# Products of each row with itself: rows at multiples of 256 bytes, and stores on two queues

## The chip, the cores and the metric

The kernel runs on one core of one Trainium2 chip. The metric is the device time of one execution in microseconds (us); where a kernel was run several times, it is their median. One further execution is taken with the hardware profiler, and the profile and its trace come from that one.

## The reference

The input `x` has 4096 rows of 256 float32 numbers. For each row, all products of two of its elements are formed, and those of the upper triangle (diagonal included) are written out, row of the triangle by row:

```python
B, D = (4096, 256)
d = inputs.shape[1]
dot = jnp.einsum('bi,bj->bij', inputs, inputs)
iu, ju = jnp.triu_indices(d)
return dot[:, iu, ju]
```

The result has 4096 rows of 256 * 257 / 2 = 32,896 float32 numbers. That is 539 MB to be written, from 4.2 MB that are read, with one multiplication per number written.

## The kernel before, in words

**Tiling.** Each of the 128 partitions takes 32 consecutive rows of `x`. They are worked on two at a time (`REPEAT`), so there are 16 groups of 128 x 2 rows. The 32,896 products of a row are cut at multiples of `UNIT` = 32 into three pieces (`PIECES`) of 10,944, 10,976 and 10,976 columns. A store thus moves one piece of one group: 128 partitions, two rows in each, 43,776 or 43,904 contiguous bytes per row. The whole work is 48 such pieces, numbered `p`; `p % 3` is the piece within the group.

**Places.** A piece is built in one of two buffers in SBUF, the places `o0` and `o1`: even `p` in the first, odd `p` in the second. Each has the form 128 x 2 x `slot`, with `slot` = 10,976, so the second row lies 43,904 bytes after the first. A place can only be refilled when its store has landed. The tile pool lays out, in this order, all of `x` (128 x 8192), `xv` (a working copy of the group's two rows, one element longer), `xa` (a copy for ScalarE), and the places.

**Who computes.** A triangle row `i` is `x[i]` times the contiguous stretch `x[i:]`, for both rows of the partition in one instruction. VectorE multiplies `xv` by `xp` (a copy of the same rows in PSUM, L220), GpSimd multiplies `xv` by itself (L272). Within a piece, GpSimd takes the tail that its cost formula puts at no more than 19.4 us (`BUDGET`), and VectorE takes the rest. `blocks` makes this division. Before the first piece of a group VectorE copies `x` into `xv` and `xp` (L199).

**The head.** The first two pieces (`AHEAD`) are shared by VectorE and ScalarE instead (L244), GpSimd being absent from them. The first piece is cut at 512, 1536, 3584 and 6400 columns (`FIRST`) and stored in five parts, so that the first transfer can begin early. ScalarE first makes its own copy `xa` (L239). Its work ends with these two pieces. From `p` = 2 on each engine runs a loop of eight passes over six pieces.

**Order of the work.** There is no scheduler; semaphores written by hand order the engines:

- SyncE issues the three loads of `x` and then, in the order of `p`, every store. Ahead of a store it waits for one increment of `v_done` (VectorE's part is done) and one of `a_done` or `g_done` (the other engine's part is done). The function is `sync`, the waits are L295 and L296, the issue is L298. All loads and stores therefore stand in one DMA queue.
- When a store has landed, the semaphore `free0` or `free1` of its place rises by 16. VectorE waits for it before it refills the place, and then releases GpSimd through `go` (L207 and L210).
- The five parts of the first piece count on `head`; TensorE waits for all of them and passes this on to `free0`.
- A group's first piece may overwrite `xv` only when GpSimd has read it (`x_read`).
- `take` (L163, L164) waits for a value and subtracts it again.

At the end SyncE waits for the last stores (L338), for `x_read` and for the three loads.

Of the kernel before, what the change touches and what calls it, by code (L numbers as in the profile page):

```python
# [1 line left out]

# [6 lines left out]
F32 = mybir.dt.float32  # L9
AF = mybir.ActivationFunctionType  # L10
ALU = mybir.AluOpType

P = 128
UNIT = 32
REPEAT = 2
PIECES = 3
PLACES = 2
SETS = 2
PASS = 6
# [94 lines left out]
def kernel(  # L114
# [15 lines left out]
    nc = tc.nc  # L130
# [12 lines left out]
    x_out = out.rearrange("(p h q r) c -> h q p r c", p=P, q=rounds, r=REPEAT)  # L143

    pool = ctx.enter_context(tc.tile_pool(name="all", bufs=1))
    xt = pool.tile([P, passes, rounds * each], F32, name="x")

    xv = pool.tile([P, each + 1], F32, name="xv")
    xa = pool.tile([P, each], F32, name="xa")

    xp = ctx.enter_context(tc.tile_pool(name="psum", bufs=1, space=bass.MemoryType.PSUM)).tile([P, each], F32, name="xp")
    places = [pool.tile([P, REPEAT, slot], F32, name=f"o{k}") for k in range(PLACES)]
    ctx.enter_context(tc.tile_critical())  # L153

    def semaphore(name: str):
        return ctx.enter_context(nc.semaphore(name))

    free = [semaphore(f"free{k}") for k in range(PLACES)]
    head, v_done, a_done, go = (semaphore(s) for s in ("head", "v_done", "a_done", "go"))
    loads = [0, each, groups // 2 * each, groups * each]  # L160
    loaded = [semaphore(f"loaded{k}") for k in range(len(loads) - 1)]

    def take(engine, sem, value: int):  # L163
        engine.wait_ge(sem, value).then_inc(sem, -value)  # L164

    v_own, a_own, g_own = (semaphore(s) for s in ("v_own", "a_own", "g_own"))
    g_done, x_read = semaphore("g_done"), semaphore("x_read")

    def x_of(h, q: int) -> bass.AP:
        return xt[:, bass.ds(h, 1), q * each : (q + 1) * each].rearrange("p o d -> p (o d)")  # L170
# [21 lines left out]
    def vector(h, pieces: range, ahead: bool, done: int = 0) -> int:  # L192
        for p in pieces:
            place = places[p % PLACES]
            if p % PIECES == 0:
                if not ahead:
                    take(nc.vector, x_read, 1)
                for to in (xv[:, :each], xp):
                    ins = nc.vector.tensor_copy(to, x_of(h, p // PIECES))  # L199
                    if done:  # L200
                        ins._wait_ge(v_own, done)
                    ins.then_inc(v_own, 1)
                    done += 1
                nc.vector.wait_ge(v_own, done)
            if not ahead:
                if use(p) < uses:
                    nc.vector.wait_ge(free[p % PLACES], 16 * use(p)).then_inc(go, 1)  # L207
                else:
                    take(nc.vector, free[p % PLACES], 16 * uses)
                    nc.vector.sem_inc(go, 1)  # L210
            for _, _, _, block, lo in blocks(p, ahead):
                order = interleave(block)

                own = (p + 1) % PIECES == 0 or p == pieces[-1]
                waits = schedule(order)
                counted = {*waits.values(), *([len(order) - 1] if own else [])}
                number = {k: done + 1 + c for c, k in enumerate(sorted(counted))}
                for k, ((i, j, at, length), m, _) in enumerate(order):
                    at -= lo
                    ins = nc.vector.tensor_tensor(  # L220
                        place[:, :, at : at + m * length],
                        window(xv[:, j:], [[d, REPEAT], [1, m], [1, length]]),
                        window(xp[:, i:], [[d, REPEAT], [1, m], [0, length]]),
                        ALU.mult,
                    )
                    if k in waits:
                        ins._wait_ge(v_own, number[waits[k]])
                    if k in counted:
                        ins.then_inc(v_own, 1)
                done += len(counted)  # L230
                if own:
                    nc.vector.wait_ge(v_own, done).then_inc(v_done, 1)
                else:
                    ins.then_inc(v_done, 1)
        return done

    def scalar(pieces: range):

        nc.scalar.activation(xa, x_of(0, 0), AF.Copy).then_inc(a_own, 1)  # L239
        take(nc.scalar, a_own, 1)  # L240
        for p in pieces:
            for _, _, block, _, lo in blocks(p, True):
                todo = [
                    nc.scalar.activation(  # L244
                        places[p][:, r, at - lo : at - lo + length],
                        xa[:, r * d + j : r * d + j + length],
                        AF.Copy,
                        scale=xa[:, r * d + i : r * d + i + 1],
                    )
                    for i, j, at, length in block  # L250
                    for r in range(REPEAT)
                ]
                if todo:
                    todo[-1].then_inc(a_done, 1)
                else:
                    nc.scalar.sem_inc(a_done, 1)

    def gpsimd(h, pieces: range, ahead: bool):

        done = turns = 0  # L260
        for p in () if ahead else pieces:
            place = places[p % PLACES]
            ((_, _, block, _, lo),) = blocks(p, False)
            turns += 1
            nc.gpsimd.wait_ge(go, turns)
            order = interleave(block)
            waits = schedule(order)
            counted = {len(order) - 1, *waits.values()}
            number = {k: done + 1 + c for c, k in enumerate(sorted(counted))}
            for k, ((i, j, at, length), m, _) in enumerate(order):  # L270
                at -= lo
                ins = nc.gpsimd.tensor_tensor(  # L272
                    place[:, :, at : at + m * length],
                    window(xv[:, j:], [[d, REPEAT], [1, m], [1, length]]),
                    window(xv[:, i:], [[d, REPEAT], [1, m], [0, length]]),
                    ALU.mult,
                )
                if k in waits:
                    ins._wait_ge(g_own, number[waits[k]])
                if k in counted:  # L280
                    ins.then_inc(g_own, 1)
            done += len(counted)
            nc.gpsimd.wait_ge(g_own, done).then_inc(g_done, 1)
            if (p + 1) % PIECES == 0:
                nc.gpsimd.sem_inc(x_read, 1)
        if turns:
            nc.gpsimd.sem_inc(g_own, -done)
            nc.gpsimd.sem_inc(go, -turns)

    def sync(h, pieces: range, ahead: bool):  # L290
        for p in pieces:
            place = places[p % PLACES]
            parts = list(blocks(p, ahead))
            for lo, hi, *_, base in parts:
                take(nc.sync, v_done, 1)  # L295
                take(nc.sync, a_done if ahead else g_done, 1)  # L296
                to = x_out[bass.ds(h, 1), p // PIECES, :, :, base + lo : base + hi]
                nc.sync.dma_start(to.rearrange("o p r c -> p (o r) c"), place[:, :, lo:hi]).then_inc(  # L298
                    free[p % PLACES] if len(parts) == 1 else head, 16
                )  # L300

    def all_pieces(engine, pieces_of):
        done = pieces_of(0, range(AHEAD), True)
        if engine is nc.vector:
            nc.vector.sem_inc(v_own, -done)
        if engine is not nc.sync:
            for sem in loaded[1:]:
                engine.wait_ge(sem, 16)
        kind = engine.engine
        with nc.Fori(  # L310
            0,
            passes,
            engines=OrderedEngineSet([kind]),
            head_slot={kind: 0} if engine is not nc.sync else {},
        ) as h:
            done = pieces_of(h, range(AHEAD, PASS), False)
            with engine.If(h < passes - 1):
                nxt = nc.s_assert_within(h + 1, 0, passes - 1)
                if engine is nc.vector:
                    nc.vector.sem_inc(v_own, -vector(nxt, range(AHEAD), False, done))  # L320
                else:
                    pieces_of(nxt, range(AHEAD), False)
        if engine is nc.vector:
            nc.vector.sem_inc(v_own, -done)
# [7 lines left out]
    take(nc.tensor, head, 16 * (len(FIRST) + 1))  # L332
    nc.tensor.sem_inc(free[0], 16)
    scalar(range(AHEAD))
    for engine, pieces_of in ((nc.vector, vector), (nc.gpsimd, gpsimd), (nc.sync, sync)):
        all_pieces(engine, pieces_of)
    for k in range(PLACES):
        take(nc.sync, free[k], 16 * uses)  # L338
    take(nc.sync, x_read, 1)
    for sem in loaded:  # L340
        take(nc.sync, sem, 16)


# [25 lines left out]
```

## Time and profile before

| | |
|---|---|
| Median of 3 runs | 1270.35 us (1270.26 to 1270.40) |
| Profiled execution: its span, first to last instruction | 1268.8 us |
| VectorE busy | 794.1 us, 63% |
| GpSimd busy | 767.8 us, 61% |
| ScalarE busy (head only) | 29.9 us, 2% |
| DMA moved | 543 MB, 428 GB/s on average |

The profiled execution is known by its span alone; no other time of it is on record. The page of a profile gives the busy time of each engine, then the span in 40 equal slices (a digit is the busy share of an engine in tenths, the line GB/s is what the DMA moved), the DMA queues, the chain of work that ended last, the costliest groups of instructions with what they waited for, and the DMA issues with the median time from issue to landing. In names such as `DVE o L220 <- DMA out_dram<-o` the first part is an engine (DVE is VectorE, POOL is GpSimd, ACT is ScalarE, SP is SyncE), what it writes and the line of the kernel, and after the arrow comes what ended its wait. Behind the page stands the trace, with a record of each instruction and of each DMA packet. In this kernel a packet of a store is one row of one partition. A table of windows gives the same busy times for chosen stretches of the span; the last two columns are the share of time in which the DMA engines were busy, and the GB/s.

### The profile page before, as it was taken

The page shows a single profiled execution, that of the slowest core. Times are in us where ns is not written, and L with a number is a line of the kernel's source. Part 1 is how long each engine was busy: PE and PEld are TensorE (multiplying, and loading weights), DVE is VectorE, ACT ScalarE, POOL GpSimd, SP SyncE. Part 2 cuts the span into 40 slices and gives each one's busy share as a digit, 9 for nine tenths or more (in the row PEclk, how much of TensorE's full clock was granted, in tenths as well). Part 3 has the DMA queues.
Part 4 walks back from the last instruction along what each step waited for, and adds up shares of the span by engine and source line. Part 5 has one row for each costly group of instructions (what it writes and reads, how often), then busy time and mean ns, then how long its engine had stood idle before and what let it go on. Part 6 is the DMA issues. An engine that isn't in the chain of part 4 may idle for free. (4 is left out here: it accounts for less than half of the span.)

```text
span 1268.8 us, 3000 instructions
## 1 busy us (share of the span) xinstructions
DVE 794.1 (63%) x1197; ACT 29.9 (2%) x80; POOL 767.8 (61%) x1032
## 2 busy tenths in 40 slices
DVE  8756856567466674766648665486655866468560
ACT  9000000000000000000000000000000000000000
POOL 0467674676647765577556765567656675576750
DMA  9999999999999999999999999999999999999997
GB/s 379 438 437 425 439 431 433 434 428 433 431 435 429 437 426 438 426 437 424 439 425 439 427 436 429 435 430 433 430 433 428 435 421 441 421 442 421 438 425 336
DMA packets 14583, 543.22 MB, mean 428 GB/s; under 512 B 880, under 2 KB 880, under 8 KB 1520
## 3 DMA queue, kind: packets, MB, share of 16 engines
q1 hardware_dynamic: 14576, 543.17, 99.5%
q14 instruction: 7, 0.06, 0.0%
HBM read 4.19 MB, written 538.97 MB: 428 GB/s over the span
## 5 line engine op out<-in xcount | busy, mean ns | idle before, releaser
L272 POOL TENSOR_TENSOR o<-xv 128x292 f32<-128x292 f32 (+60 forms) x1028 | 767.6, 787 | 461.8 <-DVEq L207 322.1
L220 DVE TENSOR_TENSOR o<-xv,xp 128x512 f32<-128x512 f32 (+61 forms) x1164 | 776.1, 746 | 429.4 <-DMA out_dram<-o 303.8
L244 ACT ACTIVATE o<-xa 128x253 f32<-128x253 f32 (+38 forms) x78 | 27.9, 454 | 0.2 <-ACTq L164 0.2
L199 DVE COPY xv<-x 128x512 f32 (+1 forms) x16 | 6.8, 427 | 10.0 <-DVEq L164 7.2
L199 DVE COPY xp<-x 128x512 f32 (+1 forms) x16 | 11.1, 695 | 0.6
L239 ACT ACT_TABLE_LOAD x1 | 1.3, 1283 | 0.9 <-SPq L153 0.9
L328 DVE MEMSET xv<- 128x1 f32 x1 | 0.1, 59 | 1.0 <-SPq L153 1.0
L239 ACT ACTIVATE xa<-x 128x512 f32<-128x512 f32 x1 | 0.6, 631 | 1.7 <-DMA x<-in_r_inputs_dram 1.7
L356 POOL MEMSET const-float32-0.0<- 128x1 f32 x1 | 0.1, 98 | 0.2 <-issue 0.2
L356 POOL MEMSET const-bfloat16-1.0<- 128x1 bf16 x1 | 0.1, 101 | 0.0
L356 POOL MEMSET const-uint8-127<- 128x1 uint8 x1 | 0.1, 101 | 0.0
L356 POOL MEMSET const-float32-1.0<- 128x1 f32 x1 | 0.1, 98 | 0.0
## 6 DMA issues: line engine op xcount, KB each, us to landing
out_dram<-o SPq DMA_DIRECT2D x32, 10976.0 KB, 32.1
out_dram<-o SPq DMA_DIRECT2D x15, 10944.0 KB, 33.6
out_dram<-o SPq DMA_DIRECT2D x1, 4544.0 KB, 19.4
out_dram<-o SPq DMA_DIRECT2D x1, 2816.0 KB, 15.1
x<-in_r_inputs_dram SPq DMA_DIRECT2D x1, 2048.0 KB, 12.4
out_dram<-o SPq DMA_DIRECT2D x1, 2048.0 KB, 12.6
x<-in_r_inputs_dram SPq DMA_DIRECT2D x1, 1792.0 KB, 7.1
out_dram<-o SPq DMA_DIRECT2D x1, 1024.0 KB, 9.7
```

The source lines that it names most:

```text
L199: ins = nc.vector.tensor_copy(to, x_of(h, p // PIECES))
L220: ins = nc.vector.tensor_tensor(place[:, :, at : at + m * length], window(xv[:, j:], [[d, REPEAT], [1, m], [1, length]]), window(xp[:, i:] ...
L239: nc.scalar.activation(xa, x_of(0, 0), AF.Copy).then_inc(a_own, 1)
L244: nc.scalar.activation(places[p][:, r, at - lo : at - lo + length], xa[:, r * d + j : r * d + j + length], AF.Copy, scale=xa[:, r * d + i ...
L272: ins = nc.gpsimd.tensor_tensor(place[:, :, at : at + m * length], window(xv[:, j:], [[d, REPEAT], [1, m], [1, length]]), window(xv[:, i:] ...
L328: nc.vector.memset(xv[:, each:], 0.0)
L356: nc = _bacc.Bacc("TRN2", target_bir_lowering=False, num_devices=1)
```

## The change

The change has these parts:

- `UNIT` goes from 32 to 64 columns, so that pieces start and end at multiples of 256 bytes: 10,944, 10,944 and 11,008 columns. `slot` becomes 11,008, so the rows of a place are 44,032 bytes apart.
- An unused tile of 32 columns, `edge`, is laid out first, then the places, then `x` and `xv`. The places with it are to start at multiples of 256 bytes.
- ScalarE's copy `xa` is dropped; in the head it reads `x` itself.
- `v_done`, `a_done` and `g_done` become two semaphores each, one per place.
- `sync` becomes `store`, which takes an engine and a place. SyncE issues the stores of the first place, ScalarE, once its part of the head is done, those of the second, on its own DMA queue. ScalarE thus also runs the loop of eight passes.
- Of the waits at the end, those for the last stores come last.

```diff
-UNIT = 32
+UNIT = 64
 REPEAT = 2
 PIECES = 3
+EDGE = 32
...
+    pool.tile([P, EDGE], F32, name="edge")
+    places = [pool.tile([P, REPEAT, slot], F32, name=f"o{k}") for k in range(PLACES)]
     xt = pool.tile([P, passes, rounds * each], F32, name="x")
-
     xv = pool.tile([P, each + 1], F32, name="xv")
-    xa = pool.tile([P, each], F32, name="xa")
...
-    places = [pool.tile([P, REPEAT, slot], F32, name=f"o{k}") for k in range(PLACES)]
...
-    head, v_done, a_done, go = (semaphore(s) for s in ("head", "v_done", "a_done", "go"))
+    head, go = semaphore("head"), semaphore("go")
+    v_done, a_done, g_done = ([semaphore(f"{s}{k}") for k in range(PLACES)] for s in ("v_done", "a_done", "g_done"))
...
-        nc.scalar.activation(xa, x_of(0, 0), AF.Copy).then_inc(a_own, 1)
-        take(nc.scalar, a_own, 1)
+        xa = xt[:, 0, :each]
...
-    def sync(h, pieces: range, ahead: bool):
+    def store(engine, k: int, h, pieces: range, ahead: bool):
         for p in pieces:
-            place = places[p % PLACES]
+            if p % PLACES != k:
+                continue
+            place = places[k]
             parts = list(blocks(p, ahead))
             for lo, hi, *_, base in parts:
-                take(nc.sync, v_done, 1)
-                take(nc.sync, a_done if ahead else g_done, 1)
+                take(engine, v_done[k], 1)
+                take(engine, (a_done if ahead else g_done)[k], 1)
                 to = x_out[bass.ds(h, 1), p // PIECES, :, :, base + lo : base + hi]
-                nc.sync.dma_start(to.rearrange("o p r c -> p (o r) c"), place[:, :, lo:hi]).then_inc(
-                    free[p % PLACES] if len(parts) == 1 else head, 16
+                engine.dma_start(to.rearrange("o p r c -> p (o r) c"), place[:, :, lo:hi]).then_inc(
+                    free[k] if len(parts) == 1 else head, 16
                 )
...
     scalar(range(AHEAD))
-    for engine, pieces_of in ((nc.vector, vector), (nc.gpsimd, gpsimd), (nc.sync, sync)):
+    stores = [(engine, partial(store, engine, k)) for k, engine in enumerate((nc.sync, nc.scalar))]
+    for engine, pieces_of in ((nc.vector, vector), (nc.gpsimd, gpsimd), *stores):
         all_pieces(engine, pieces_of)
-    for k in range(PLACES):
-        take(nc.sync, free[k], 16 * uses)
     take(nc.sync, x_read, 1)
     for sem in loaded:
         take(nc.sync, sem, 16)
+    for k in range(PLACES):
+        take(nc.sync, free[k], 16 * uses)
```

More of the change, by code (lines that the diff above doesn't have):

```diff
@@ L1 @@
 from contextlib import ExitStack
+from functools import partial
 import concourse.bass as bass
@@ L164, in take @@
         engine.wait_ge(sem, value).then_inc(sem, -value)
-    v_own, a_own, g_own = (semaphore(s) for s in ("v_own", "a_own", "g_own"))
-    g_done, x_read = semaphore("g_done"), semaphore("x_read")
+    v_own, g_own = (semaphore(s) for s in ("v_own", "g_own"))
+    x_read = semaphore("x_read")
     def x_of(h, q: int) -> bass.AP:
@@ L231, in vector @@
                 if own:
-                    nc.vector.wait_ge(v_own, done).then_inc(v_done, 1)
+                    nc.vector.wait_ge(v_own, done).then_inc(v_done[p % PLACES], 1)
                 else:
-                    ins.then_inc(v_done, 1)
+                    ins.then_inc(v_done[p % PLACES], 1)
         return done
     def scalar(pieces: range):
-        nc.scalar.activation(xa, x_of(0, 0), AF.Copy).then_inc(a_own, 1)
-        take(nc.scalar, a_own, 1)
+        xa = xt[:, 0, :each]
         for p in pieces:
@@ L253, in scalar @@
                 if todo:
-                    todo[-1].then_inc(a_done, 1)
+                    todo[-1].then_inc(a_done[p % PLACES], 1)
                 else:
-                    nc.scalar.sem_inc(a_done, 1)
+                    nc.scalar.sem_inc(a_done[p % PLACES], 1)
     def gpsimd(h, pieces: range, ahead: bool):
@@ L282, in gpsimd @@
             done += len(counted)
-            nc.gpsimd.wait_ge(g_own, done).then_inc(g_done, 1)
+            nc.gpsimd.wait_ge(g_own, done).then_inc(g_done[p % PLACES], 1)
             if (p + 1) % PIECES == 0:
@@ L305, in all_pieces @@
             nc.vector.sem_inc(v_own, -done)
-        if engine is not nc.sync:
+        if engine in (nc.vector, nc.gpsimd):
             for sem in loaded[1:]:
@@ L313, in all_pieces @@
             engines=OrderedEngineSet([kind]),
-            head_slot={kind: 0} if engine is not nc.sync else {},
+            head_slot={kind: 0} if engine in (nc.vector, nc.gpsimd) else {},
         ) as h:
```

## The prediction

> **What bounds the kernel now.** I read the page first (busy shares, slices, queues), then the table of windows, the DMA view of the last 89 us, the waits and the chain.
>
> ```profile
> DMA  9999999999999999999999999999999999999997
> ...
> q1 hardware_dynamic: 14576, 543.17, 99.5%
> ...
> out_dram<-o SPq DMA_DIRECT2D x32, 10976.0 KB, 32.1
> ```
>
> The 16 DMA engines are busy in every slice; VectorE and GpSimd have about 40% of the span free. A store takes about 26 us of transfer, yet 32 to 34 from issue to landing: it is issued some 6 us before the one ahead of it is through, and lines up behind it. The compute can get slower by nearly that much and cost nothing.
>
> ```profile
> 0.00:41.00 41.00, 33.22 (x48) 29.86 (x80) 0.20 (x4) 1.00 0.97 393
> 41.00:119.00 78.00, 49.40 (x74) 0.00 (x0) 50.20 (x66) 1.00 1.00 433
> 119.00:430.00 311.00, 197.60 (x296) 0.00 (x0) 200.79 (x264) 1.00 1.00 433
> 430.00:950.00 520.00, 331.14 (x499) 0.00 (x0) 333.70 (x446) 1.00 1.00 432
> 950.00:1185.00 235.00, 148.20 (x222) 0.00 (x0) 150.59 (x198) 1.00 1.00 430
> ```
>
> The last two columns are the DMA share and the GB/s: full throughout, 433 at first, 430 late. The next view cuts 1180 us to the end into 40 slices of 2.2 us:
>
> ```profile
> GB/s 336 612 316 335 611 316 454 493 335 611 316 335 611 316 336 613 316 554 396 316 633 316 336 613 316 336 613 316 336 613 316 336 613 336 613 316 336 20 20 0
> ```
>
> ```profile
> DVE o L220 <- DMA out_dram<-o: 303.8, 31, 12.3
> ...
> DVE o L220 <- DVEq L164: 119.2, 14, 12.4
> ```
>
> At the end there are two slices of 20 GB/s, less than one engine's share. I followed that to the packet records of the trace (one packet is one row of one partition, 43,776 or 43,904 bytes; 16 rows per engine and store; 4-byte packets mark where an engine is through with a store). One engine is late: it ends each late store 4.4 us after the median engine (1.4 us at the first full store, 2.1 at 380 us, 4.4 from 920 us on). It ends the last one at 1266.79 and the span ends at 1268.76. A place is refilled only when this engine has landed its rows, so **the time is the row count of the late engine**: from 40.7 us on, 47 stores of 16 rows, 752 rows in 1226.1 us, 1630 ns per row.
>
> ```profile
> 1215.22 19.92 DVE o L220 x39
> ```
>
> This last piece of the chain gives the other half of the cycle: landing to next issue is G = 20.3 us for the piece with index 2 (19.92 and its waits), 18.2 for index 0 and 17.9 for index 1 (GpSimd, 17.93 and 17.70 in the timeline).
>
> **What the Trainium skill says.** "DMA: Bandwidth & Descriptors", section "Where 436 GB/s comes from": a ceiling of 435.2 GB/s. The trace agrees: its shortest rows follow each other every 1619 ns (43,904 bytes) or 1614 ns (43,776), 434 GB/s over 16 engines. The same page, "How a descriptor splits into AXI transactions": a transfer that doesn't start at a multiple of 256 bytes first fetches from the boundary below. That is at most one more transaction of 256 bytes a row. The same page, "Queues, rings and completion order": each engine alternates between the queues it has work for, a packet at a time. One queue carries all stores here, so no row of this trace shows it. "Issuing engines are not separate DMA queues" of that page: several issuing engines save only issue time.
>
> **The change, part by part.**
>
> *Addresses.* Rows of the result are 131,584 bytes, 514 x 256. Before, piece 2 begins at 87,680 (342.5 x 256) and the second row of a place lies 43,904 (171.5 x 256) after the first, so of the two rows of a partition at least one starts off a multiple. After, all do. Price by the skill, an estimate: at most 256 bytes more per row, at 27.2 bytes per ns 9.4 ns, on 752 rows 7.1 us. The trace speaks against it: in the first full stores the rows of most engines take 1622 ns each, one like the other, both rows of a partition, in piece 1 (which starts on a multiple) as in piece 2 (which doesn't). Shorter than these the rows won't get. So the other end is what lies between the late engine's rows and the shortest: 752 rows at the shortest are 32 x 16 x 1.619 + 15 x 16 x 1.614 = 1216.3 us, 9.8 less than now. Most of these 9.8 us don't look like addresses. On the late engine from 1111 us on the mean excess of a row over the shortest is 26 ns while the two compute engines work through piece 2 (77 instructions), 11 ns in piece 0 (26), 9 ns in piece 1 (35), and 3.4 ns after the last compute instruction: it goes with instructions, whatever the rows' addresses. What addresses could still take away is the 3.4: 752 x 3.4 = 2.6 us. The other engines have 5 ns, in piece 0 5.6 and 3.3 by row, so alignment may touch part of it. I take half: **-1.3 us**, range 0 to -9.8; a loss is excluded as no transfer gets more bytes.
>
> *Pieces.* 32 columns pass from piece 1 to piece 2, 0.3% of a piece, under 0.1 us of compute, beside slack of 4 to 6 us: 0. If that slack were gone, 0.1 us for each of 16 stores, 1.6.
>
> *ScalarE's copy.* Its copy (0.63 us) and wait (0.2) go, so its head work ends at 31.8 instead of 32.7. VectorE's ends at 37.1, and the first store parts queue behind the loads until 14.0 us: 0. Without that cover 0.8.
>
> *Two queues.* All stores of place 1, with their waits and DMA issues (0.37 us each on SyncE), move to ScalarE, behind its head work only. On both engines nothing but the next store is queued behind a waiting instruction. The issue price is taken as the same; a us more would fall into the slack. Semaphores by place replace shared ones, one increment for one: 0.
>
> What changes is the order of rows. Let w = 26.1 us be a store's work on the late engine and left(n) what it still owes of store n-1 when the rows of n arrive. With one queue, n waits; left is always s = w - 0.65 (landing, 1214.55 to 1215.2) - G - 1.0 (issue to first packet, from the first load): 4.1, 6.2, 6.4 us for next pieces 2, 0, 1. The trace has 4.4, 6.1 and 6.4. With two queues taking turns row by row, n-1 lands left(n) later, but by then n has had the same time done. So left(n+1) = s - left(n): nothing is lost unless that is negative. From left = 0 ahead of a piece-0 store it runs 6.2, 0.2, 3.9, 2.3, 4.1, 0.0 and repeats every six stores: never below zero, but at zero once.
>
> The start loses. The rows of store 1 arrive at 38.3, when the late engine still has 3 or 4 rows (0.67 us each) of the first piece to 40.7. Between them go long rows: the first piece lands 3.2 to 4.9 us later. Store 2's compute now starts at 43.58, 2.5 us after that landing was seen (41.1), so some of it may be absorbed. Store 2's rows then arrive at 66.3 to 69.9; the engine's work on store 1 ends at 67.3 as before. Idle: 0 to 2.6, I take **+1.3**; the waits then absorb it, it isn't repeated.
>
> A switch between queues: no row shows one. Nearest, the row at which the next store is issued is some 43 ns longer. Some 3.4 rows of each store are in company, 160 switches: 0 to +6.9 us; below zero, hiding the 5 ns by which even a shortest row exceeds its bytes at 27.2, -0.8. I take 0, as rows of neighbouring stores on one queue show no gap either.
>
> *The end.* Four of SyncE's closing waits now precede the last landing, 17 ns each: -0.1.
>
> Sum: -1.3 + 1.3 - 0.1 = -0.1 on the span of 1268.8, so 1268.7. The profiled execution has no time beside its span; the median of 1270.35 is 1.55 above it, which I carry over: about **1270.2**.
>
> **The rivals.**
>
> *Rows at their shortest (faster).* If the late engine's excess comes from addresses, all 9.8 us go: 1260.6; with half, 1265.4. For it: the excess exists in loaded stretches only, where misplaced rows could cost bursts. Against it: the shortest rows are misplaced too, and the excess follows the compute.
>
> *Turns of several rows (slower).* At the arrival of a store the engine may give its queue k rows before it returns to the older one. Then the old store lands 1.63k later, and left(n+1) = s - 1.63k: from k = 3 (4.9) below the 4.1 of piece 2, at k = 4 (6.5) below all three, by 2.4, 0.3 and 0.1. The next store then finds nothing ahead of it, so it happens at every second store: for k = 4 0.93 x 23 = 21 us, 1291; for k = 3 0.8 at some 8 to 16 stores, 6 to 13, about 1279. It decides from three rows on. For it: packets of many descriptors are what the skill calls typical. Against it: the trace has one packet per row.
>
> *A switch costs 43 ns* (slower): +6.9, 1277.
>
> *The places don't come to lie at multiples*, or that is worth nothing: 1271.5, within the first case.
>
> **How the numbers follow.** This kernel's measurement tells 0.2%, 2.5 us, from no change. My forecast (1268 to 1272.8): 0.45. Shorter rows, below 1267.8: 0.27. Turns of three rows or more: 0.20, switch price: 0.08, together slower 0.28. The range leaves out the lower half of the shorter rows (below 1264) and the turns of four and more (above 1277.5), about 0.1 each.
>
> **What would show it.** Right: the late engine still lags by about 4 us; rows in the loaded stretches stay near 1627 and 1630 ns; the two queues carry half the bytes each; rows alternate singly where stores overlap; issue to landing spreads to 31 to 36 us; one gap near 67 us. Wrong: rows at 1618 to 1622 in late stretches and a rate of 433 to 434 GB/s to the end (faster); DMA gaps at every second store (turns); longer rows wherever two stores overlap (switch).

## The result, and the profile after

The changed kernel takes 1273.83 us (median of 19 runs, 1269.02 to 1275.32), the kernel before 1270.37 us in the runs beside them (1270.18 to 1270.63). The ratio is 1.0022, with an interval of 1.0016 to 1.0027: slower by 0.2%, where 1270.2 had been predicted. Its runs spread over 6 us, those of before over half a microsecond. A trace shows one run only; that of the changed kernel is of a run of 1273.98 us. Three sets of lines answer to those of before. The first are lines of the page of the changed kernel: DMA share in 40 slices, queues, and the most frequent issues.

```profile
DMA  9999999999999999999999999999999999999998
...
q1 hardware_dynamic: 8048, 273.68, 50.0%
q10 hardware_dynamic: 6528, 269.49, 49.5%
...
out_dram<-o ACTq DMA_DIRECT2D x16, 10944.0 KB, 32.9
out_dram<-o SPq DMA_DIRECT2D x15, 10944.0 KB, 32.5
```

The change did what it says: the stores are halved between SyncE's queue (q1) and ScalarE's (q10). The engines still count as busy all the time, so a loss has to be in the rows themselves. The second set is the table of windows of the changed kernel, with the same cuts as before (last columns: DMA share, GB/s).

```profile
41.00:119.00 78.00, 49.46 (x74) 0.00 (x0) 50.09 (x66) 1.00 1.01 432
119.00:430.00 311.00, 197.87 (x296) 0.00 (x0) 200.36 (x264) 1.00 1.00 431
430.00:950.00 520.00, 331.64 (x499) 0.00 (x0) 333.05 (x446) 1.00 1.00 429
950.00:1185.00 235.00, 148.40 (x222) 0.00 (x0) 147.94 (x196) 1.00 1.00 429
```

Compute is unchanged; the rate is lower than before in every stretch, 429 instead of 432 GB/s between 430 and 950 us. The third set is VectorE's two waits for landed stores (total us, times, longest) in the changed kernel.

```profile
DVE o L222 <- DMA out_dram<-o: 291.2, 31, 13.8
...
DVE o L222 <- DVEq L166: 137.0, 14, 18.1
```

Their sum is 428 us, as before (423), but the longest is 18.1 instead of 12.4: landings are no longer evenly spaced.

The packet records show two opposite effects. (They name no engine: rows are put down to one engine where one begins as the other ends.) Nine in ten rows now take exactly the shortest time, 1618 ns (43,776 bytes) or 1627 (44,032). Against that, 145 rows are longer by more than 200 ns, most by 0.7 to 1.1 us, 7.5 us per engine in all. Nearly every one is the first row that an engine takes of a new store, just after its last row of the older store on the other queue. Here are one engine's rows from 1178 us on (S: SyncE's queue, A: ScalarE's, whose store was issued at 1187.6):

```
S 1627 1627 1627 1627 1627 1627 1627   A 2481 1618 1618 1618
```

The late engine is still there. It ends its last store at 1270.64 us, 1.9 us after the median engine; in the kernel before it was 1266.79, 4.3 us after.

### The profile page after: what moved, and what is told of

Read it like the earlier page. It is cut to its first block, busy times and chain, and to the rows that moved or that the text cites. A ratio compares the mean times of both kernels' runs of the same rounds, so it can differ in the third digit from the quotient of the medians.

```text
span 1272.2 us, 3047 instructions
## 1 busy us (share of the span) xinstructions
DVE 795.1 (63%) x1197; ACT 29.2 (2%) x79; POOL 766.1 (60%) x1032
## 5 line engine op out<-in xcount | busy, mean ns | idle before, releaser
L245 ACT ACTIVATE o<-x 128x253 f32<-128x253 f32 (+38 forms) x78 | 28.0, 454 | 0.0
## 6 DMA issues: line engine op xcount, KB each, us to landing
out_dram<-o SPq DMA_DIRECT2D x1, 2048.0 KB, 12.9
```

What stands on the lines that cost most here:

```text
L245: nc.scalar.activation(places[p][:, r, at - lo : at - lo + length], xa[:, r * d + j : r * d + j + length], AF.Copy, scale=xa[:, r * d + i ...
```

## The experiments

**The two parts apart.** Each of these kernels holds one part of the change. In the first, one queue:

```diff
...
-    stores = [(engine, partial(store, engine, k)) for k, engine in enumerate((nc.sync, nc.scalar))]
+    stores = [(nc.sync, partial(store, nc.sync))]
```

> All addresses of the change, but every store issued by SyncE on one queue, as before. Theory (the addresses shorten the rows, the second queue costs some 10 us): rows of 43,776 bytes at 1618 ns and of 44,032 at 1627 throughout, no late engine, 40.8 + 1216.4 + 2 us of span, so about 1261 us. Rival (the second queue makes the rows uniform, the addresses do nothing): rows near 1624 to 1630 ns and about 1270 us.

Measured: 1267.8 us (1267.67 to 1268.0), ratio to before 0.9980 (0.9972 to 0.9988). Rows are at 1618 and 1627 ns with one queue, so the addresses do that. But the time fell by 2.6 us only, not by 9. Two views show why: the windows, and the DMA view of 1180 us to the end, in 40 slices.

```profile
119.00:430.00 311.00, 197.82 (x296) 0.00 (x0) 200.36 (x264) 1.00 1.00 434
430.00:950.00 520.00, 331.56 (x499) 0.00 (x0) 333.04 (x446) 1.00 1.00 432
950.00:1185.00 235.00, 148.37 (x222) 0.00 (x0) 150.27 (x198) 1.00 0.99 430
```

```profile
GB/s 436 493 335 611 316 335 611 316 454 493 335 611 316 335 611 316 454 493 316 631 316 335 611 316 337 615 317 337 615 317 337 615 337 476 456 337 20 20 0 4
```

The rate starts at 434, that of the shortest rows, and falls back to 430; at the end one engine is still alone for two slices at 20 GB/s. Fifteen engines got faster and then wait for the late one, which ends each store 4.3 to 4.8 us after the median engine from 770 us on. Its time per three stores fell from 78.32 to 78.17 us. That is the gain.

The second kernel has the old addresses (`UNIT` = 32, no `edge`, the old order of tiles with `xa`) and the stores of the change on two queues:

> The two queues alone, with pieces, places and rows at the addresses of before. Theory: rows near 1627 ns as before, and in addition rows longer by some 850 ns where the engines pass from one queue to the other: about 1280 us (1270.4 plus the 8 to 14 us by which the changed kernel lies above shortest rows). Rival: uniform rows of 1618 and 1622 ns, about 1274 us as the changed kernel.

Measured: 1271.13 us (1270.65 to 1272.71), ratio 1.0007 (0.9999 to 1.0015): 0.7 us above the kernel before, which the interval doesn't tell from none; both expectations missed. It has 148 long rows, as many as the changed kernel, and yet they cost next to nothing (the trace is of its fastest run, 1270.65). The parts thus don't add: -2.6 and +0.7 would give 1268.5, and the change has 1273.8. The second queue costs 6.0 us with the new addresses.

Where these 6.0 us arise can be read from the landings. The table has how much later a store landed in the trace of the changed kernel than in that of the same addresses on one queue. It takes stores that had (nearly) landed before the rows of the next one came, so that sharing the engines with it didn't delay them.

| Store `p` | 6 | 12 | 18 | 24 | 30 | 36 | 42 | 47 |
|---|---|---|---|---|---|---|---|---|
| later by, us | 0.2 | 0.5 | 1.5 | 2.4 | 3.3 | 4.2 | 5.1 | 6.0 |

The start has cost almost nothing by store 6. After store 12 some 0.9 us are lost once in every six stores, six times in all.

**Which addresses.** Two kernels on one queue, each with half of the alignment. The first keeps the rows' offsets in the result at a multiple of 128 bytes only, with aligned places:

```diff
-UNIT = 64
+UNIT = 32
...
-    slot = max(b - a for a, b in spans)
+    slot = -(-max(b - a for a, b in spans) // 64) * 64
```

> One queue; places and their rows start at multiples of 256 bytes in SBUF, but the pieces are cut as before (10,944, 10,976 and 10,976 columns), so piece 2 starts at 342.5 x 256 bytes of a row of the result. Theory a (the addresses read in SBUF count): about 1261 us, as with all addresses. Theory b (the addresses written in HBM count): near 1270 us, with piece 2 or pieces 1 and 2 longer.

The second has aligned rows in the result, and places whose rows start 160 and 32 bytes past a multiple:

```diff
-EDGE = 32
+EDGE = 72
...
-    slot = max(b - a for a, b in spans)
+    slot = max(b - a for a, b in spans) + 32
```

> One queue; pieces cut at multiples of 256 bytes of the result, but the places start 160 bytes past a multiple and their rows are 172.5 x 256 bytes apart, as the remainders were before (160 and 32). Theory a (the addresses read in SBUF count): near 1270 us with the uneven rows of before. Theory b (the addresses written count): about 1261 us.

Measured: source aligned 1270.29 us (ratio 0.9999, 0.9991 to 1.0008), result aligned 1267.77 (0.9979, 0.9971 to 0.9987). The addresses in the result bring the whole gain. The rows tell a different story, which is worth noting: with the source aligned most rows are at the shortest 1618 and 1622 ns, with the result aligned most are not (two thirds of those of 43,776 bytes take 1622 or more). What shortens the rows of fifteen engines is the source; what shortens those of the engine that sets the time is the result. A third kernel moves the inner borders so that both of them, not one, lie half a multiple off:

```diff
-    borders = even_borders(0, width, PIECES)
+    borders = [0, 10976, 21920, width]
```

> One queue, places and their rows aligned in SBUF, inner borders of the pieces at 10,976 and 21,920 columns, so that each of the three pieces starts or ends half a multiple of 256 bytes off in the result (with the borders of before it is two of three: 1270.3 us; with none 1267.8). If what the late engine loses is by row that is off at either end: a third more, about 1271.5 us. If only starts (or only ends) count, the pieces off go from one to two: about 1272.8 us.

Measured: 1272.71 us (1272.48 to 1272.85), ratio 1.0018 (1.0011 to 1.0025): the loss doubles, so it goes by borders and not by pieces. (This total alone would fit starts alone, or ends alone, as well.) The late engine's three stores take 78.17 us with no border off, 78.32 with one, 78.48 with two. By piece (0, 1, 2), less the shortest rows, its stores take 0.16, 0.29, 0.08 us more with no border off; 0.16, 0.36, 0.17 with the second off; 0.23, 0.44, 0.17 with both. So an end that is off costs about 0.07 us a store and a start 0.09; over the two, 0.15 us for 32 rows, that is about 4.7 ns per row each.

**What makes the late engine late.** The prediction had read that its rows get longer with the number of compute instructions. This kernel (one queue, all aligned) adds instructions that do nothing for the result:

```diff
...
+                if not ahead and p % PIECES != 2:
+                    for e in range(40):
+                        nc.vector.memset(pad[:, 0, e : e + 1], 0.0)
...
+            if p % PIECES == 2:
+                for e in range(40):
+                    nc.gpsimd.memset(pad[:, 1, e : e + 1], 0.0)
```

> All addresses aligned, one queue, and in each piece of the loop 40 memsets of one column more (by VectorE in pieces 0 and 1, by GpSimd in piece 2, where each has time to spare), so no store is issued later. Theory (the late engine's rows lose about 2.1 ns for each compute instruction begun meanwhile): 46 x 40 x 2.1 ns = 3.9 us more than with the same addresses on one queue, about 1271.7 us. Rival (the lateness has to do with the engine's own rows and places): 1267.8 us, no change.

Measured: 1272.21 us (1272.01 to 1272.38), 4.4 above the same kernel without them. The late engine's three stores take 78.46 us instead of 78.17, 2.4 ns for each of the 120 added instructions. Lines of its page and of its windows:

```profile
DVE 828.3 (65%) x2397; ACT 29.2 (2%) x79; POOL 788.0 (62%) x1672
```

```profile
119.00:430.00 311.00, 206.70 (x616) 0.00 (x0) 205.83 (x424) 1.00 1.00 434
430.00:950.00 520.00, 345.99 (x1019) 0.00 (x0) 342.56 (x726) 1.00 0.99 430
```

The first stretch still has 434 GB/s: fifteen engines are untouched. The fall to 430 sets in earlier, when their lead over the late engine is used up.

**When the second queue costs.** A fifth of each piece is left uncomputed in the loop (and one memset fills the last columns of the places at the start), on two queues and on one:

```diff
-                yield a - lo, b - lo, block[k:], block[:k], lo
+                yield a - lo, b - lo, block[k : k + (len(block) - k) * 4 // 5], block[: k * 4 // 5], lo
```

> The changed kernel with a fifth of the rows of each piece left uncomputed in the loop by VectorE and by GpSimd (the stores are the same), so each store is issued some 3 to 4 us earlier. Theory (the second queue costs only where a store is issued so late that the other queue has run to its last 2 to 3 us): no long rows on the late engine, about 1267 us, level with the same kernel on one queue. Rival (passing between queues, or ScalarE's queue, costs at every store): still some 6 us above the same kernel on one queue, about 1273 us.

> All addresses aligned, one queue, and the same fifth of each piece left uncomputed: the control. On one queue the earlier issue brings nothing. If rows of the late engine lose about 2.1 ns for each compute instruction begun meanwhile, a fifth fewer gives about 0.9 us: 1266.9 us. If they don't depend on instructions: 1267.8 us.

Measured: 1266.82 us on two queues (ratio to before 0.9981, 0.9974 to 0.9988), 1266.55 on one (0.9970, 0.9957 to 0.9982). In the median the 6 us are gone. It isn't that long rows are gone: 85 remain, 4.1 us per engine. In this trace, late in the run, the late engine still has 5.5 us or more of its old store when a new one is issued, and none of the long rows is its own: its six stores take 156.17 us, against 156.16 on one queue. But the trace is of a run of 1266.62 us, and of the twenty two-queue runs eight lie between 1268.67 and 1270.75, the others below 1266.9. The fifth fewer instructions shorten the one-queue time by 1.25 us (0.9 expected).

**Is it the alternation, or ScalarE's queue?** First, each store of the loop is cut by its two rows, one half issued by SyncE and one by ScalarE after a signal from it:

```diff
...
+                r = 0 if engine is nc.sync else 1
+                engine.dma_start(to[:, r : r + 1, :], place[:, r : r + 1, lo:hi]).then_inc(free[k], 16)
```

> All addresses aligned; each store of the loop is cut by the two rows of a partition, one half issued by SyncE and one by ScalarE right after it, so both queues always hold work of the same store. Theory (alternation is free, only a store that arrives late on the other queue costs): rows alternate all the time, no long rows, about 1268 us. Rival (each passage from one queue to the other costs): some 700 passages per engine, far above 1275 us.

Measured: 1270.77 us (1270.49 to 1270.86), 3.0 above one queue, and neither of the two expectations. The engines alternate row by row for the whole run, with three rows that are over 200 ns longer than the shortest. Passing between queues as such makes no row long. The 3 us are of another kind: the late engine takes 78.29 us for three stores instead of 78.17, some 2 us in all, with nearly twice as many semaphore packets and more instructions (which of the two it is was not tried); the first full stores lose another 0.8 us in a gap. Second, all stores by ScalarE on one queue (the lines are against the kernel on SyncE's queue):

```diff
-    stores = [(nc.sync, partial(store, nc.sync))]
+    stores = [(nc.scalar, partial(store, nc.scalar))]
...
```

> All addresses aligned, and every store issued by ScalarE instead of SyncE, on one queue. If ScalarE's queue or its issue is slower by itself, this lies above the same kernel on SyncE's queue (1267.8 us), by up to the 6 us that the changed kernel loses. If the loss needs two queues, it is 1267.8 us, with no long rows beyond the start.

Measured: 1284.12 us (1284.0 to 1284.24). The expectation had overlooked the head: ScalarE computes its share of the first two pieces first and issues the first store only at 29.2 us, so the DMA engines stand still. The windows of this kernel show that this is all:

```profile
0.00:41.00 41.00, 33.15 (x48) 29.23 (x79) 0.20 (x4) 1.00 0.53 214
...
950.00:1185.00 235.00, 148.96 (x223) 0.00 (x0) 150.83 (x199) 1.00 1.00 430
```

The first piece is through at 58.1 us instead of 40.8; from then on three stores of the late engine take 78.17 us, as on SyncE's queue. ScalarE's queue is not slower by itself.

**Which turnarounds cost.** A turnaround is the time from the landing that frees a place to the issue of its next store. The same two kernels with other values of `BUDGET`, which moves work between GpSimd and VectorE and so changes the turnarounds:

> The changed kernel with the number BUDGET at 21.5 instead of 19.4: GpSimd gets more of each piece, so that pieces 0 and 1 are issued some 1.4 to 1.7 us later after a landing and piece 2 some 1.1 us earlier, 2.0 us later over three stores. Theory (on two queues a store issued late costs the late engine a long row or a gap): more of them, above the changed kernel's 1273.8 us, some 1276 to 1282. Rival (the 6 us of the second queue don't depend on when a store is issued): 1273.8 us.

> The control: all addresses aligned, one queue, BUDGET at 21.5. On one queue each store still comes 3 us or more before the late engine is through with the one ahead, so nothing changes: 1267.8 us.

Measured with 21.5: two queues 1268.05 us (1267.91 to 1269.68; ratio 0.9983, 0.9977 to 0.9990), one queue 1267.91. My theory, that later issue costs more, falls. There are 134 long rows, 6.8 us per engine, nearly as many as in the changed kernel, but the last engine doesn't pay: six stores land in 156.36 us, as on one queue. The others lose their lead and nothing else. Then more unequal turnarounds, and another start:

> The changed kernel with BUDGET at 17.0: GpSimd gets less, so the time from landing to issue is some 16, 16.5 and 21.5 us for pieces 0, 1 and 2 (18.2, 17.9 and 20.3 in the changed kernel), shorter in sum but more unequal. Theory (unequal turnarounds bring the late engine to its long rows): as the changed kernel or above, 1274 us or more, with the late engine's six stores at 157.2 us or more. Rival (the phase set at the start decides, whatever the turnarounds): anywhere from 1268 to 1275, and not tied to the inequality. Third (later issue costs more): below 1270 us; the run with BUDGET 21.5 speaks against this one already.

> The control: all addresses aligned, one queue, BUDGET at 17.0. Stores of pieces 2 are issued about 1.2 us later than with 19.4, still ahead of the late engine: 1267.8 us.

> The changed kernel, but the first store of place 1 (p = 1) is issued by SyncE behind the parts of the first piece, so the two queues first meet at p = 3; all turnarounds as in the changed kernel. Theory (unequal turnarounds decide): near 1273.8 us less the 1 to 2 us of the start. Rival (the phase set at the start decides): near 1268 us, with no long rows on the late engine, or at another level than 1273.8.

The last of these gives place 1's first store to SyncE:

```diff
-            if p % PLACES != k:
+            at = p % PLACES
+            if (0 if ahead else at) != k:
                 continue
...
```

Measured: with 17.0, two queues 1272.43 us (1270.54 to 1273.45; ratio 1.0014, 1.0006 to 1.0023) and one queue 1267.94; with the other start 1275.35 (1274.42 to 1275.52). The trace with 17.0 is of a run of 1270.95 us; six stores take 156.4 and 156.7 us by turns in it, and not the 157.2 expected. With the other start the late engine is back at 157.26 us for six stores, exactly the changed kernel's 157.25, so what sets this repeated loss isn't the phase at the start. (The total is higher, as 1.9 us are lost by store 13 already.) The loss differs with the turnarounds of the three pieces: 0.1, 6.0 and 4.5 us above one queue for 21.5, 19.4 and 17.0. That it grows with their inequality is not borne out, as the most unequal lies in the middle. Nor do the turnarounds decide alone: the kernel with the queues alone has those of the changed kernel to about 0.1 us and loses next to nothing, and runs of the changed kernel itself lie anywhere from 1269.02 to 1275.32.

## Why the prediction was wrong, step by step

**The bound.** Right, and it carried further than I used it: the time is the row count of the late engine times its row. Fifteen engines gained up to 0.35 us per three stores from the aligned source, and the time didn't move. The late engine's dependence on instructions, read from the trace of before as 26, 11 and 9 ns by piece, was borne out in kind by adding some (2.4 ns each).

**Addresses: -1.3 us, measured -2.6.** The mechanism, gain and place were right, the size half. 2.6 was the number worked out for the whole of what the late engine shows without compute, and I took half of it, because rows of the first stores looked alike on and off a multiple. Those were rows of engines that are not late. On the late engine an off start or end costs about 4.7 ns a row. By the Trainium skill ("DMA: Bandwidth & Descriptors", "How a descriptor splits into AXI transactions") a transfer that starts 128 bytes past a multiple fetches those 128 bytes in vain; at the prediction's 27.2 bytes per ns that is an estimate of 4.7 ns. The measurement has this size, but not in this place: the section speaks of what is read, and here starts off in SBUF, where a store reads, did not change the time (1267.77 us), while starts off in the result did. It shows the same for an end, which the section doesn't charge.

**Two queues: +1.3 us at the start and nothing after. This is the step that failed.** Measured is +6.0 against the same addresses on one queue. In the prediction's words, "the waits then absorb it, it isn't repeated", and of the switch: "I take 0, as rows of neighbouring stores on one queue show no gap either".

Its picture of the order was right. Rows alternate singly, so the slower rival with turns of several rows didn't happen, and the rests ran nearly as forecast. (The rest is what the late engine still has to do of the older store when the next one is issued.) At the last six stores of the changed kernel the older store took another 12.9, 2.5, 8.4, 5.6, 9.1 and 1.9 us. Less the 1 us from issue to first packet, and halved because two stores share the engine, this is an estimate of 5.9, 0.8, 3.7, 2.3, 4.0 and 0.5 us of work; the prediction's chain had 6.2, 0.2, 3.9, 2.3, 4.1 and 0.0. (Its own terms give s = 6.55 for piece 1 and not 6.4, which changes little.) That this cycle came was partly luck: with the other start it runs three stores shifted, and with the queues alone the rests settle evenly, at 8.7, 5.6, 5.3, 8.8, 5.7 and 5.3 us late in the run.

Wrong is that a low rest costs nothing until it is negative. At store 47, after a rest of 1.9 us, the first row of the other queue is 0.98 us longer on the late engine. A rest that low comes once in six stores, which take 157.25 us instead of 156.34. From store 17 on that is six times 0.9 us; before it only about 0.5 us are lost. So the start, put at 1.3, was put too high, and what repeats was put at nothing. With the queues alone, where no rest is below 5.3 us late in the run, six stores take 156.66 us, as in the kernel before (156.65). The sentence of the Trainium skill that the prediction took up, that several issuing engines save only issue time ("DMA: Bandwidth & Descriptors", "Issuing engines are not separate DMA queues"), has no such cost; the measured 6.0 us decide.

When a first row gets long shows in the six traces in which whole stores alternate between the queues. Of 481 first rows that began 1.2 to 2.0 us after the issue of their store, 480 were over 200 ns too long; of 3054 that began 2.4 us after it or later, none was. An engine that had run dry began about 1.0 us after the issue, mostly with a gap and not with a long row. So a long row needs an engine that is just finishing the older store.

**The switch price.** The rival had 43 ns at each of 160 switches, 6.9 us, and 1277: near the time, by another mechanism. It is rare and twenty times as large: most switches are free, and most of those 1.2 to 2.0 us after an issue cost 0.7 to 1.1 us.

**Pieces, the end.** The compute slack of 4 to 6 us is there on one queue: with `BUDGET` at 17.0, 19.4 and 21.5 it takes 1267.94, 1267.8 and 1267.91 us. ScalarE's copy and the order of the last waits were not tried alone.

**What stays open.** Why a first row gets long in that stretch of time, why the rests settle into a cycle that has a low one for the late engine in some kernels and runs and not in others, and which requests make one engine late with each instruction (the profiler's own recording was not ruled out). No run tells these. The version that beats both kernels is the change on one queue, 1267.8 us.

## What to carry to other kernels

When all engines of a pool must finish before the next step can start, look for the one that is always last: what the other fifteen gain is lead, and not time. A second queue turns a line into a sharing. Work that waited its turn at no cost now arrives beside the older store, delays its landing, and needs a margin of its own. So judge it by what each store still has to do when the next is issued, and try alignment and queues apart, as their sum was not the result.

## What the runs showed of the hardware that wasn't expected

- With stores alternately on two queues, a store's first row on a DMA engine was mostly 0.7 to 1.1 us longer where it began 1.2 to 2.0 us after the issue, as the engine finished the older store (480 of 481 were over 200 ns too long), and never from 2.4 us on (0 of 3054). With both queues filled at the same time (rows alternating all the run) three rows of 12,032 were over 200 ns too long, as many as on one queue.
- One of the 16 engines lost 2.4 ns for each VectorE or GpSimd instruction begun meanwhile, memsets of one column included; over the first stretch all 16 together still had 434 GB/s.
- A row whose start or end in the result lay 128 bytes off a multiple of 256 cost that engine about 4.7 ns at each such edge.
